# Cross-attention on one core: the attention product in seven block products, the softmax maximum as a bias

## The chip, the core and the metric

The kernel runs on one core of a Trainium2 chip. The metric is the device time of one execution in microseconds. Before the change the median of three runs is 286.38 us (286.36 to 286.68).

The engines are named as the profile names them: PE (TensorE, matmuls; PEld its weight loads), DVE (VectorE), ACT (ScalarE), POOL (GpSimd), SP (SyncE, which issues the DMAs). Each engine works through its own instructions in the order of the program and waits where an operand isn't ready.

## The reference

Everything is in fp32. There are 16 batches of 256 queries (width 256) and 77 keys (width 192), 8 heads of width 256. The output has the shape of x.

```python
Q = (img_embed @ Wq).reshape(B, -1, H, D).transpose(0, 2, 1, 3)
K = (sent_embed @ Wk).reshape(B, -1, H, D).transpose(0, 2, 1, 3)
V = (sent_embed @ Wv).reshape(B, -1, H, D).transpose(0, 2, 1, 3)
score = jnp.einsum('bhqd,bhkd->bhqk', Q, K) / math.sqrt(D)
score = jnp.where(mask, score, -jnp.inf)
attn = jax.nn.softmax(score, axis=-1)
ctx = jnp.einsum('bhqk,bhkd->bqhd', attn, V).reshape(B, -1, H * D)
out = ctx @ Wo + img_embed
mu = jnp.mean(out, axis=-1, keepdims=True)
var = jnp.var(out, axis=-1, keepdims=True)
return (out - mu) * jax.lax.rsqrt(var + EPS) * gamma + beta
```

## The kernel before

The weights are multiplied with each other first. Per head, g = Wk Wq^T (tiles gA and gB, the key width 192 split into 128 and 64 rows) and u = Wv Wo (uA and uB). With the keys' inputs c, a = g c gives the scores as x a, and vw = c u gives the output as a sum over heads of p vw. So the attention product of one batch is a matrix p of 256 queries by 8 x 77 keys times a matrix of 8 x 77 rows by 256 columns. Of each head 64 keys go into four blocks of 128 rows (two heads' halves to a block; the array runs in column strips of 32), and the 13 last keys of all heads go into a fifth block, vr.

After a preparation of some 57 us a loop runs over b from -1 to 15, one step for each batch, as a pipeline by hand: in step b the two query tiles (of 128 queries) of batch b + 1 are "new", those of batch b are "now", those of batch b - 1 are "old". Each engine's order is the program's:

- `scores(t)` (L297), PE: x times a for a new tile, 32 groups of four matmuls of 154 columns over two tiles (two records each, as fp32 goes through in two passes).
- `finish(t)` (L374, L376, L379), DVE: adds the product in PSUM to x and takes mean and variance. `spread` (L387), ACT: the root. `invert` (L394), DVE: its reciprocal.
- `shift(t)` (L311, L318, L319): DVE adds the mask's bias to the scores and takes the maximum `top`; POOL subtracts the maximum.
- `exponential(t)` (L326), ACT: one activation for a tile of 8 x 77. Root and exponential need different tables, so each step has two table loads on ACT.
- `prepare_vw(b + 1)` (L225, L236) and, in the steps up to b = 10, `prepare_a` for a part of the next group of four batches (L184, L198), PE; their copies from PSUM to SBUF are ACT's (L752, L754).
- `weigh(t)` (L332, L334, L340): DVE sums the exponentials and inverts the sum, POOL multiplies.
- `normalise(t)` (L416, L419), DVE; from the twelfth step on partly ACT and POOL instead (L412 to L414). Then SP sends the result (L427).
- `transpose_x` (L160), DVE, in two steps of each group of four; `turn_last` (L287), DVE, in the first half of the loop.
- `attend(t)` (L362), PE: the product for a "now" tile, five blocks by four strips of 256 columns. `turn(t)` (L350), DVE, transposes p of the new tiles for the next step's product.

All PSUM tiles share eight banks; a matmul into a bank waits until its last reader is done.

Of the kernel before, what the change touches and what calls it, by code (L numbers as in the profile page):

```python
# [8 lines left out]
F32 = mybir.dt.float32  # L9
# [6 lines left out]
P = 128  # L16
H = 8
D = 256
EPS = 1e-05
GB = 4  # L20
KM = 64
MASKED = 3.0e38

# [19 lines left out]
def kernel(  # L45
# [51 lines left out]

    gB = const.tile([P, NF, DI], F32, tag="gB", name="gB")

    uA = const.tile([P, 2, DI // BK, NF, BK], F32, tag="uA", name="uA")  # L100
    uB = const.tile([P, 2, DI // BK, NF, BK], F32, tag="uB", name="uB")

    cA = const.tile([P, B, S2], F32, tag="cA", name="cA")
    cB = const.tile([P, B, S2], F32, tag="cB", name="cB")
# [110 lines left out]

    def prepare_vw(b):

        vw_of[b] = vwp.tile([P, 2, 2, DI], F32, tag="vw", name=f"vw_{b}", bufs=3)
        pv = []

        def part_A():
            for k in range(2):
                pv.append(ps_mm.tile([P, 2 * DI], F32, tag="mm", name=f"pv_{b}_{k}"))
                for i in range(NM):
                    nc.tensor.matmul(  # L225
                        pv[k][i * BK : (i + 1) * BK],
                        cA[:, b, k * BK : (k + 1) * BK],
                        uA[:, :, :, i],
                        start=True,
                        stop=False,  # L230
                    )

        def part_B():
            for i in range(NM):
                for k in range(2):
                    nc.tensor.matmul(  # L236
                        pv[k][i * BK : (i + 1) * BK],
                        cB[half(k), b, k * BK : (k + 1) * BK],
                        uB[half(k), :, :, i],
                        start=False,  # L240
                        stop=True,
                    )

        def copies():
            return [
                (vw_of[b][:, :, k, :], pv[k].rearrange("p (e d) -> p e d", e=2)) for k in range(2)
            ]

        return part_A, part_B, copies

    def prepare_last():


        pr = [ps_mm.tile([P, 2, B, KR], F32, tag="mm", name=f"pr_{n}") for n in range(DI // BK)]

        def part_A(e):
            for n, o in enumerate(pr):
                nc.tensor.matmul(  # L258
                    o[:, e].rearrange("p b k -> p (b k)"),
                    flat(uA[:, e, n]),  # L260
                    flat(cRA),
                    start=(e == 0),
                    stop=(e == 1),
                )

        def part_B(e):
            for n, o in enumerate(pr):
                nc.tensor.matmul(  # L268
                    o[:, e].rearrange("p b k -> p (b k)"),
                    flat(uB[half(n % 2), e, n]),  # L270
                    flat(cRB[half(n % 2)]),
                    start=(e == 1),
                    stop=(e == 0),
                )

        part_A(0)
        part_B(0)
        part_B(1)
        part_A(1)
        for n, o in enumerate(pr):  # L280
            to = vr[:, :, n * BK : n * BK + 2 * KR]
            evacuate(to.rearrange("p b (e k) -> p e b k", e=2), o)
# [22 lines left out]

    def shift(t):

        b, ps = t // QT, ps_of.pop(t)
        s = sp.tile([P, H, S2], F32, tag="s", name=f"s_{t}")
        for a in range(2):  # L310
            nc.vector.tensor_tensor(  # L311
                s[:, a * H // 2 : (a + 1) * H // 2],
                ps[a][:, : H // 2 * S2].rearrange("p (h k) -> p h k", k=S2),
                bias[:, b, :].unsqueeze(1).to_broadcast([P, H // 2, S2]),
                ALU.add,
            )
        top = st.tile([P, H], F32, tag="top", name=f"top_{t}")
        nc.vector.tensor_reduce(top, s, AX.X, ALU.max)  # L318
        nc.gpsimd.tensor_tensor(  # L319
            s, s, top.unsqueeze(2).to_broadcast([P, H, S2]), ALU.subtract  # L320
        )
        s_of[t] = s

    def exponential(t):
        e = sp.tile([P, H, S2], F32, tag="e", name=f"e_{t}")
        nc.scalar.activation(e, s_of.pop(t), AF.Exp)  # L326
        e_of[t] = e

    def weigh(t):
# [27 lines left out]
    def attend(t):  # L357
        b, pT = t // QT, pT_of.pop(t)
        po = ps_mm.tile([P, DI], F32, tag="mm", name=f"po_{t}")
        for n in range(NF + 1):  # L360
            for i in range(NM):
                nc.tensor.matmul(  # L362
                    po[i * BK : (i + 1) * BK],
                    pT[:, n, i],
                    vw_of[b][:, n // 2, n % 2, :] if n < NF else vr[:, b, :],
                    start=(n == 0),
                    stop=(n == NF),
                )
        po_of[t] = po

    def finish(t):
        g, j = t // GT, t % GT
        y = xg_of[g][:, j, :]
        nc.vector.tensor_tensor(y, po_of.pop(t), y, ALU.add)  # L374
        bn = st.tile([P, 6], F32, tag="bn", name=f"bn_{t}")
        nc.vector.bn_stats(bn, y)  # L376
        if j == 0:
            mv_of[g] = st.tile([P, GT, 2], F32, tag="mv", name=f"mv_{g}", bufs=2)
        nc.vector.bn_aggr(mv_of[g][:, j, :], bn)  # L379
# [54 lines left out]
    with tc.tile_pool(name="wonce", bufs=1) as wp:  # L434
# [247 lines left out]
        for j in range(NF // 2):  # L682
            pu = two_banks("pu", j)
            for a in range(2 * j, 2 * j + 2):
                of_pair(pu, a, wv_part, wo_part)
            for e in range(2):
                evacuate(
                    uA[:, e, :, 2 * j : 2 * j + 2].rearrange("p n a c -> p a n c"),
                    pu[e].rearrange("p a (n c) -> p a n c", c=BK),
                )  # L690
        for j in range(NF // 2):
            for e, pw in enumerate(
                rest_of_pairs(j, (2 * j, 2 * j + 1), wv_part, wo_part, "pw")
            ):
                for i, engine in enumerate((nc.scalar.copy, nc.vector.tensor_copy)):
                    a = 2 * j + i
                    here, there = uB[half(i), e, :, a], uB[half(1 - i), e, :, a]
                    engine(here, pw[half(i)].rearrange("p (n c) -> p n c", c=BK))
                    nc.gpsimd.tensor_copy(there, here)
        nan = wp.tile([P, B, 1], F32, tag="nan", name="nan")  # L700
        nc.vector.tensor_reduce(nan[:, :, 0], bias, AX.X, ALU.max)
        nc.gpsimd.tensor_tensor(nan, nan, nan, ALU.mult)
# [16 lines left out]
    for b in range(-1, B):  # L719
        old = range(max(b - 1, 0) * QT, b * QT)  # L720
        now = range(max(b, 0) * QT, (b + 1) * QT)
        new = range((b + 1) * QT, min(b + 2, B) * QT)
        for t in new:
            scores(t)
        if old and new:
            for t in old:
                finish(t)
            spread(old[0], old[-1] + 1)
        for t in new:
            shift(t)  # L730
        for n in range(0, 2) if b < 0 else range(b + 2, min(b + 3, B // 2)):
            turn_last(n)
        if old and new:
            invert(old[0], old[-1] + 1, aside=b >= B - GB - 1)
        g, n = (b + 1) // GB + 1, (b + 1) % GB
        work = []
        if b + 1 < B:
            work.append(prepare_vw(b + 1))
        if g < NG:
            work.append(prepare_a(g, (n,)))  # L740
            if n == 0:
                load_xT(g)
                load_x(g)
        for part_A, _, _ in work:
            part_A()
        for _, part_B, _ in work:
            part_B()
        copies = [copy for _, _, of_part in work for copy in of_part()]
        for i, t in enumerate(new):
            exponential(t)  # L750
            for dst, src in copies[i : i + 1]:
                nc.scalar.copy(dst, src)  # L752
        for dst, src in copies[len(new) :]:
            nc.scalar.copy(dst, src)  # L754
        for i, t in enumerate(new):
            weigh(t)
            if old and b < B - 2 and (i or b < B - GB - 1):
                normalise(old[i])
        if g < NG and n >= NF - 2:
            for j in range((n - NF + 2) * GT // 2, (n - NF + 3) * GT // 2, 2):  # L760
                transpose_x(g, j)
        for t in now:
            attend(t)
        for t in new:
            turn(t)
        if B - GB - 1 <= b < B - 2:
            normalise(old[0], aside=True)
        if b == B - 2:
            for i in range(QT):
                normalise(old[i], aside=True)  # L770
                finish(now[i])
            spread(now[0], now[-1] + 1)
# [43 lines left out]
```

## Time and profile before

| | |
|---|---|
| median of 3 runs | 286.38 us |
| the profiled execution | 285.98 us |
| its span, first to last instruction | 284.2 us |
| granted PE clock | 0.996 |
| first scores of the loop, on PE | 57.30 us |
| step b = 1 begins on PE | 82.10 us |
| step b = 11 begins on PE | 226.97 us |
| scores of the last batch end on PE | 265.28 us |
| a step of b = 1 to 10, PE | 14.49 us |
| a step of b = 11 to 13, PE | 11.38 us |

The span is divided by the chain of work into a preparation (to 57.3 us), seventeen steps and a tail of some 16 us after 268.1, in which the last tiles go through exponential, product and normalisation one after the other.

A row of the groups of instructions reads: line, engine, operation, output <- inputs, shapes, count, then busy time, the mean of one in ns, and the idle time before them with what ended it. A row of the stretches reads: stretch, length, and then busy time and count for PE, PEld, DVE, ACT and POOL.

### The profile page before, as it was taken

The page shows a single profiled execution, that of the slowest core. Times are in us where ns is not written, and L with a number is a line of the kernel's source. Part 1 is how long each engine was busy: PE and PEld are TensorE (multiplying, and loading weights), DVE is VectorE, ACT ScalarE, POOL GpSimd, SP SyncE. Part 2 cuts the span into 40 slices and gives each one's busy share as a digit, 9 for nine tenths or more (in the row PEclk, how much of TensorE's full clock was granted, in tenths as well). Part 3 has the DMA queues.
Part 4 walks back from the last instruction along what each step waited for, and adds up shares of the span by engine and source line. Part 5 has one row for each costly group of instructions (what it writes and reads, how often), then busy time and mean ns, then how long its engine had stood idle before and what let it go on. Part 6 is the DMA issues. An engine that isn't in the chain of part 4 may idle for free.

```text
span 284.2 us, 11523 instructions
## 1 busy us (share of the span) xinstructions
PE 274.4 (97%) x5221; PEld 180.2 (63%) x5221; DVE 215.3 (76%) x421; ACT 115.2 (41%) x199; POOL 119.1 (42%) x150
## 2 busy tenths in 40 slices
PE   8999999999999999999999999999999999999990
PEld 7746599976474747575656565666656567476550
DVE  0245953775777989988888888897978898898883
ACT  3303222214362444453535353535353534725541
POOL 1000069524515252525252434352533437748574
PEclk9999999999999999999999999999999999999998
DMA  6997999960000105920101039301010101010112
GB/s 211 229 224 174 325 213 225 155 142 2 2 6 2 40 2 102 189 86 5 39 2 40 2 81 193 105 2 39 3 39 5 40 3 39 2 42 3 39 40 74
DMA packets 35634, 22.51 MB, mean 79 GB/s; under 512 B 17712, under 2 KB 34048, under 8 KB 35584
## 3 DMA queue, kind: packets, MB, share of 16 engines
q1 hardware_dynamic: 35584, 21.77, 34.8%
q8 instruction: 41, 0.67, 1.0%
q14 instruction: 9, 0.07, 0.1%
HBM read 17.57 MB, written 4.19 MB: 77 GB/s over the span
## 4 chain that ended last, share of the span: by engine, by line
PE 93%; DVE 2%; POOL 1%; ACT 1%; issue 1%; POOLq 0%
PE ps L297 24%; PE po L362 22%; PE pa L184 12%; PE pv L225 10%; PE pa L198 6%; PE pv L236 6%; PE pu L568 3%; PE pr L258 2%; PE pg L611 1%; PE idle L493 1%; PE pw L582 1%; PE pgb L568 1%; PE pr L268 1%; PE pc L545 1%; PE phb L582 1%; PE ph L625 1%
## 5 line engine op out<-in xcount | busy, mean ns | idle before, releaser
L319 POOL TENSOR_TENSOR s<-s,top 128x616 f32<-128x616 f32 x32 | 38.9, 1216 | 90.5 <-DVE top L318 86.0
L297 PE MATMUL ps<-a,xT 128*32 128x154 f32 x2048 | 70.0, 294 | 0.0
L297 PEld LDWEIGHTS ps<-a,xT 128*32 128x32 f32 x2048 | 66.4, 110 | 3.5 <-issue 0.7
L340 POOL TENSOR_TENSOR p<-e,rden 128x512 f32<-128x512 f32 x64 | 50.1, 802 | 31.8 <-ACT a L754 27.0
L362 PE MATMUL po<-vw,pT 128*32 128x256 f32 x1024 | 61.5, 380 | 0.0
L362 PEld LDWEIGHTS po<-vw,pT 128*32 128x32 f32 x1024 | 31.8, 110 | 28.2 <-issue 5.5
L332 DVE TENSOR_REDUCE den<-e 128x8 f32<-128x616 f32 x32 | 25.3, 790 | 23.6 <-ACT e L326 23.6
L184 PE MATMUL pa<-cA,gA 128*32 128x308 f32 x512 | 35.8, 423 | 0.4 <-ACT cA L136 0.4
L326 ACT ACTIVATE e<-s 128x616 f32<-128x616 f32 x32 | 23.0, 719 | 28.7 <-POOL s L319 28.7
L752 ACT COPY vw<-pv 128x512 f32<-128x512 f32 x32 | 18.6, 581 | 36.1 <-PE pv L236 36.1
L311 DVE TENSOR_TENSOR s<-ps,bias 128x308 f32<-128x308 f32 x64 | 27.8, 465 | 4.1 <-PE ps L297 4.1
L225 PE MATMUL pv<-uA,cA 128*32 128x512 f32 x256 | 30.4, 592 | 0.0
L184 PEld LDWEIGHTS pa<-cA,gA 128*32 128x32 f32 x512 | 16.4, 110 | 21.1 <-issue 6.1
L419 DVE SCALAR_TENSOR_TENSOR xg<-xg,rstd,bet 128x256 f32<-128x256 f32 x25 | 27.9, 1117 | 0.9
L387 ACT ACTIVATE std<-mv,eps 128x2 f32<-128x2 f32 (+1 forms) x17 | 5.0, 296 | 55.1 <-DVE mv L379 54.3
L350 DVE STREAM_TRANSPOSE pT<-p 128x640 f32<-128x640 f32 x32 | 25.0, 811 | 2.5 <-POOL p L340 2.5
L318 DVE TENSOR_REDUCE top<-s 128x8 f32<-128x616 f32 x32 | 25.5, 796 | 1.1
L362 PE MATMUL po<-vr,pT 128*32 128x256 f32 x256 | 19.7, 379 | 0.0
L198 PE MATMUL pa<-cB,gB 64*32 64x308 f32 x512 | 19.5, 420 | 0.0
L387 ACT ACT_TABLE_LOAD x15 | 19.2, 1283 | 0.3
L326 ACT ACT_TABLE_LOAD x14 | 18.0, 1283 | 0.3
L236 PE MATMUL pv<-uB,cB 64*32 64x512 f32 x256 | 17.4, 601 | 0.0
(86 smaller groups left out, 272.2 us busy)
## 6 DMA issues: line engine op xcount, KB each, us to landing
xT<-in_x_dram SPq DMA_DIRECT2D x16, 256.0 KB, 7.4
xg<-in_x_dram SPq DMA_DIRECT2D x4, 1024.0 KB, 9.0
out_dram<-xg SPq DMA_DIRECT2D x15, 256.0 KB, 2.2
wo<-in_L_xattn_Wo_dram SPq DMA_DIRECT2D x4, 512.0 KB, 5.4
wvT<-in_L_xattn_Wv_dram SPq DMA_DIRECT2D x16, 96.0 KB, 3.9
wq_nat<-in_L_xattn_Wq_dram SPq DMA_DIRECT2D x2, 512.0 KB, 6.1
wq_blk<-in_L_xattn_Wq_dram SPq DMA_DIRECT2D x8, 128.0 KB, 4.4
wk_blk<-in_L_xattn_Wk_dram SPq DMA_DIRECT2D x8, 96.0 KB, 5.8
```

The lines of the kernel that those rows point to most:

```text
L184: nc.tensor.matmul(flat(o[i * BK : (i + 1) * BK]), gA[:, h, cols(dc, i)], flat(cA[:, batches, :]), start=not B_first, stop=B_first,)
L198: nc.tensor.matmul(flat(banks[j + k][i * BK : (i + 1) * BK]), gB[half(k), h % NF, cols(dc, i)], flat(cB[half(k), batches, :]), start=B_fir ...
L225: nc.tensor.matmul(pv[k][i * BK : (i + 1) * BK], cA[:, b, k * BK : (k + 1) * BK], uA[:, :, :, i], start=True, stop=False,)
L236: nc.tensor.matmul(pv[k][i * BK : (i + 1) * BK], cB[half(k), b, k * BK : (k + 1) * BK], uB[half(k), :, :, i], start=False, stop=True,)
L297: nc.tensor.matmul(ps[m // 2][i * BK : (i + 1) * BK, m % 2 * 2 * S2 : (m % 2 + 1) * 2 * S2], xT_of[g][:, j * NM + m, dc], flat(a_of[g][:, ...
L311: nc.vector.tensor_tensor(s[:, a * H // 2 : (a + 1) * H // 2], ps[a][:, : H // 2 * S2].rearrange("p (h k) -> p h k", k=S2), bias[:, b, :]. ...
L318: nc.vector.tensor_reduce(top, s, AX.X, ALU.max)
L319: nc.gpsimd.tensor_tensor(s, s, top.unsqueeze(2).to_broadcast([P, H, S2]), ALU.subtract)
L326: nc.scalar.activation(e, s_of.pop(t), AF.Exp)
L340: nc.gpsimd.tensor_tensor(part, e_mh[:, :, :, keys], rden_mh.unsqueeze(3).to_broadcast(list(part.shape)), ALU.mult,)
L362: nc.tensor.matmul(po[i * BK : (i + 1) * BK], pT[:, n, i], vw_of[b][:, n // 2, n % 2, :] if n < NF else vr[:, b, :], start=(n == 0), stop= ...
L419: nc.vector.scalar_tensor_tensor(y, y, rstd, bet, ALU.mult, ALU.add)
```

## The change

For the batches 0 to 10 (b < NS, NS = 11) the product of p and vw is done in the form of Strassen (Winograd's variant). p of a batch is seen as two query tiles by two halves of the blocks, vw as two halves of the blocks by two halves of the 256 columns. In place of eight block products of 128 columns there are seven, plus products with the fifth block vr, which are added to four of them in PSUM. The sums that the form needs are made so: the one for the right-hand side, `t2`, comes out of the projection, since uA and uB get a fifth slice with the sum of slices (four additions on POOL in the preparation); the differences `ts` and `vd` of vw and vr (`differences`) and the four sums of p (`sums`) are POOL's in each step; the products land in two PSUM tiles, pm and po, and `add_seven` has ACT copy pm to SBUF and POOL add it to x in five additions. The second query tile's `finish` then reads only 128 columns from PSUM.

For the tiles of batches 0 to 11 the maximum is taken with its sign turned and goes in as the bias of the exponential, which so becomes eight activations of 77 columns, one for each head; POOL's subtraction is left out there.

The steps b < 11 have an order of their own: each old tile's `finish` stands ahead of a new tile's `shift`, the root comes after both exponentials, the copies after the root, the transpositions of x between the two `weigh`, and DVE normalises the first old tile before `turn` and the second after it. The later steps are as before. No DMA is added or taken away.

```diff
-    uA = const.tile([P, 2, DI // BK, NF, BK], F32, tag="uA", name="uA")
-    uB = const.tile([P, 2, DI // BK, NF, BK], F32, tag="uB", name="uB")
+    NH = DI // 2 // BK
+    uA = const.tile([P, 5, NH, NF, BK], F32, tag="uA", name="uA")
+    uB = const.tile([P, 5, NH, NF, BK], F32, tag="uB", name="uB")
+    NS = B - GB - 1
...
     def prepare_vw(b):
-        vw_of[b] = vwp.tile([P, 2, 2, DI], F32, tag="vw", name=f"vw_{b}", bufs=3)
+        vw_of[b] = vwp.tile([P, 4, 2, P], F32, tag="vw", name=f"vw_{b}", bufs=3)
+        parts = slice(0, 4) if b < NS else slice(1, 5)
...
-                        uA[:, :, :, i],
+                        uA[:, parts, :, i],
...
     def shift(t):
...
-        nc.vector.tensor_reduce(top, s, AX.X, ALU.max)
-        nc.gpsimd.tensor_tensor(
-            s, s, top.unsqueeze(2).to_broadcast([P, H, S2]), ALU.subtract
-        )
-        s_of[t] = s
+        nc.vector.tensor_reduce(top, s, AX.X, ALU.max, negate=t // QT <= NS)
+        if t // QT > NS:
+            nc.gpsimd.tensor_tensor(
+                s, s, top.unsqueeze(2).to_broadcast([P, H, S2]), ALU.subtract
+            )
+        s_of[t] = s, top
 
     def exponential(t):
         e = sp.tile([P, H, S2], F32, tag="e", name=f"e_{t}")
-        nc.scalar.activation(e, s_of.pop(t), AF.Exp)
+        s, top = s_of.pop(t)
+        if t // QT > NS:
+            nc.scalar.activation(e, s, AF.Exp)
+        else:
+            for h in range(H):
+                nc.scalar.activation(e[:, h], s[:, h], AF.Exp, bias=top[:, h : h + 1])
         e_of[t] = e
...
+    def differences(b):
+        vw = vw_of[b].rearrange("p q k d -> p q (k d)")
+        ts = vwp.tile([P, 3, 2, P], F32, tag="ts", name=f"ts_{b}", bufs=2)
+        nc.gpsimd.tensor_tensor(
+            ts.rearrange("p q k d -> p q (k d)"),
+            vw[:, 1:4],
+            vw[:, 0:1].to_broadcast([P, 3, 2 * P]),
+            ALU.subtract,
+        )
+        vd = vwp.tile([P, P], F32, tag="vd", name=f"vd_{b}", bufs=2)
+        nc.gpsimd.tensor_tensor(vd, vr[:, b, :P], vr[:, b, P:], ALU.subtract)
+        ts_of[b] = ts, vd
+
+    def sums(b):
...
+        ss = vwp.tile([P, 4, 2, NM, BK], F32, tag="ss", name=f"ss_{b}", bufs=2)
+        s1, s3, s2, s4 = (ss[:, i].rearrange("p k m q -> p (k m q)") for i in range(4))
+        nc.gpsimd.tensor_tensor(s1, a2[0], a2[1], ALU.add)
+        nc.gpsimd.tensor_tensor(s3, a2[0], a1[0], ALU.subtract)
+        nc.gpsimd.tensor_tensor(s2, a2[1], s3, ALU.add)
+        nc.gpsimd.tensor_tensor(s4, a1[1], s2, ALU.subtract)
+        ss_of[b] = ss
+
+    def seven(b):
...
+        contract(pm[:, 0], pT[0][:, 0:2], b11)
+        contract(pm[:, 1], s2, t2)
+        contract(pm[:, 2], s3, t3, (pT[1][:, NF], ends[1]))
+        contract(pm[:, 3], s1, t1)
+        contract(po[:, 0], pT[0][:, 2:4], b21, (pT[0][:, NF], ends[0]))
+        contract(po[:, 1], s4, b22, (pT[0][:, NF], ends[1]))
+        contract(po[:, 2], pT[1][:, 2:4], t4, (pT[1][:, NF], vd))
+        po_of[QT * b] = flat(po[:, 0:2]), slice(None)
+        po_of[QT * b + 1] = po[:, 2], slice(P)
+        pm_of[b] = pm
+
+    def add_seven(b):
+        m = vwp.tile([P, 4, P], F32, tag="m", name=f"m_{b}", bufs=1)
+        nc.scalar.copy(m, pm_of.pop(b))
+        j = QT * b % GT
+        y = xg_of[QT * b // GT][:, j : j + QT].rearrange("p t (c d) -> p t c d", c=2)
+
+        def add(to, what):
+            nc.gpsimd.tensor_tensor(to, to, what, ALU.add)
+
+        add(m[:, 1], m[:, 0])
+        add(y[:, 0], m[:, 0:2])
+        add(y[:, :, 1], m[:, 3:4].to_broadcast([P, QT, P]))
+        add(m[:, 2], m[:, 1])
+        add(y[:, 1], m[:, 2:3].to_broadcast([P, 2, P]))
...
+        for u in (uA, uB):
+            t2, _, b22, b11, b12 = (u[:, q].rearrange("p n i c -> p (n i c)") for q in range(5))
+            nc.gpsimd.tensor_tensor(t2, b22, b12, ALU.subtract)
+            nc.gpsimd.tensor_tensor(t2, t2, b11, ALU.add)
...
+        if b < NS:
+            for i, t in enumerate(new):
+                if old:
+                    finish(old[i])
+                shift(t)
...
+        if b < NS:
+            for i, t in enumerate(new):
+                exponential(t)
+                if i and old:
+                    spread(old[0], old[-1] + 1)
+                weigh(t)
+                if i == 0 and n >= NF - 2:
+                    for j in range((n - NF + 2) * GT // 2, (n - NF + 3) * GT // 2, 2):
+                        transpose_x(g, j)
+            for dst, src in copies:
+                nc.scalar.copy(dst, src)
+            if b + 1 < NS:
+                differences(b + 1)
+            if now:
+                seven(b)
+                add_seven(b)
+            if old:
+                invert(old[0], old[-1] + 1)
+                normalise(old[0])
+            for t in new:
+                turn(t)
+            if b + 1 < NS:
+                sums(b + 1)
+            if old:
+                normalise(old[1])
+            continue
```

`contract(out, weights, moving, ...)` issues, for each block of 128 rows, four matmuls of 128 columns, one for each strip of 32 columns of the array.

More of the change, by code (lines that the diff above doesn't have):

```diff
@@ L98, with of_e @@
     gB = const.tile([P, NF, DI], F32, tag="gB", name="gB")
-    uA = const.tile([P, 2, DI // BK, NF, BK], F32, tag="uA", name="uA")
-    uB = const.tile([P, 2, DI // BK, NF, BK], F32, tag="uB", name="uB")
+    NH = DI // 2 // BK
+    uA = const.tile([P, 5, NH, NF, BK], F32, tag="uA", name="uA")
+    uB = const.tile([P, 5, NH, NF, BK], F32, tag="uB", name="uB")
+    NS = B - GB - 1
+    def of_e(u, e):
+        return u[:, 3 - 2 * e : 5 - 2 * e].rearrange("p q n i c -> p (q n) i c")
     cA = const.tile([P, B, S2], F32, tag="cA", name="cA")
@@ L238, in part_B @@
                         cB[half(k), b, k * BK : (k + 1) * BK],
-                        uB[half(k), :, :, i],
+                        uB[half(k), parts, :, i],
                         start=False,
@@ L245, in copies @@
             return [
-                (vw_of[b][:, :, k, :], pv[k].rearrange("p (e d) -> p e d", e=2)) for k in range(2)
+                (vw_of[b][:, :, k, :], pv[k].rearrange("p (q d) -> p q d", q=4)) for k in range(2)
             ]
@@ L259, in part_A @@
                     o[:, e].rearrange("p b k -> p (b k)"),
-                    flat(uA[:, e, n]),
+                    flat(of_e(uA, e)[:, n]),
                     flat(cRA),
@@ L269, in part_B @@
                     o[:, e].rearrange("p b k -> p (b k)"),
-                    flat(uB[half(n % 2), e, n]),
+                    flat(of_e(uB, e)[half(n % 2), n]),
                     flat(cRB[half(n % 2)]),
@@ L364, in attend @@
                     pT[:, n, i],
-                    vw_of[b][:, n // 2, n % 2, :] if n < NF else vr[:, b, :],
+                    vw_of[b][:, 2 - n // 2 * 2 : 4 - n // 2 * 2, n % 2, :] if n < NF else vr[:, b, :],
                     start=(n == 0),
@@ L368, in attend @@
                 )
-        po_of[t] = po
+        po_of[t] = po, slice(None)
+    def differences(b):
[10 more added lines that the diff above has]
+        ts_of[b] = ts, vd
@@ new lines, in sums @@
+    def sums(b):
+        a1, a2 = (
+            [flat(pT_of[QT * b + i][:, 2 * e : 2 * e + 2].rearrange("p n m q -> p n (m q)"))
+             for e in range(2)]
+            for i in range(QT)
+        )
+        ss = vwp.tile([P, 4, 2, NM, BK], F32, tag="ss", name=f"ss_{b}", bufs=2)
[5 more added lines that the diff above has]
+        ss_of[b] = ss
@@ new lines, in seven, with contract @@
+    def seven(b):
+        pT = [pT_of.pop(QT * b + i) for i in range(QT)]
+        vw, ss = vw_of[b], ss_of.pop(b)
+        ts, vd = ts_of.pop(b)
+        pm = ps_mm.tile([P, 4, P], F32, tag="mm", name=f"pm_{b}")
+        po = ps_mm.tile([P, 3, P], F32, tag="mm", name=f"po_{b}")
+        t2, b21, b22, b11 = (vw[:, q] for q in range(4))
+        t4, t1, t3 = (ts[:, q] for q in range(3))
+        s1, s3, s2, s4 = (ss[:, i] for i in range(4))
+        ends = vr[:, b, :P], vr[:, b, P:]
+        def contract(out, weights, moving, *last):
+            terms = [(weights[:, k], moving[:, k]) for k in range(2)] + list(last)
+            for n, (weight, moving) in enumerate(terms):
+                for i in range(NM):
+                    nc.tensor.matmul(
+                        out[i * BK : (i + 1) * BK],
+                        weight[:, i],
+                        moving,
+                        start=(n == 0),
+                        stop=(n == len(terms) - 1),
+                    )
+        contract(pm[:, 0], pT[0][:, 0:2], b11)
[8 more added lines that the diff above has]
+        pm_of[b] = pm
@@ L371, in finish @@
+    ts_of, ss_of, pm_of = {}, {}, {}
     def finish(t):
@@ L373, in finish @@
         y = xg_of[g][:, j, :]
-        nc.vector.tensor_tensor(y, po_of.pop(t), y, ALU.add)
+        po, cols = po_of.pop(t)
+        nc.vector.tensor_tensor(y[:, cols], po, y[:, cols], ALU.add)
         bn = st.tile([P, 6], F32, tag="bn", name=f"bn_{t}")
@@ L687 @@
                 evacuate(
-                    uA[:, e, :, 2 * j : 2 * j + 2].rearrange("p n a c -> p a n c"),
+                    of_e(uA, e)[:, :, 2 * j : 2 * j + 2].rearrange("p n a c -> p a n c"),
                     pu[e].rearrange("p a (n c) -> p a n c", c=BK),
@@ L696 @@
                     a = 2 * j + i
-                    here, there = uB[half(i), e, :, a], uB[half(1 - i), e, :, a]
+                    here, there = (of_e(uB, e)[half(k), :, a] for k in (i, 1 - i))
                     engine(here, pw[half(i)].rearrange("p (n c) -> p n c", c=BK))
                     nc.gpsimd.tensor_copy(there, here)
+        for u in (uA, uB):
+            t2, _, b22, b11, b12 = (u[:, q].rearrange("p n i c -> p (n i c)") for q in range(5))
+            nc.gpsimd.tensor_tensor(t2, b22, b12, ALU.subtract)
+            nc.gpsimd.tensor_tensor(t2, t2, b11, ALU.add)
         nan = wp.tile([P, B, 1], F32, tag="nan", name="nan")
@@ L724 @@
             scores(t)
-        if old and new:
+        if b < NS:
[3 more added lines that the diff above has]
+                shift(t)
+        elif new:
             for t in old:
@@ L728 @@
             spread(old[0], old[-1] + 1)
-        for t in new:
-            shift(t)
+            for t in new:
+                shift(t)
         for n in range(0, 2) if b < 0 else range(b + 2, min(b + 3, B // 2)):
             turn_last(n)
-        if old and new:
-            invert(old[0], old[-1] + 1, aside=b >= B - GB - 1)
+        if b >= NS and new:
+            invert(old[0], old[-1] + 1, aside=True)
         g, n = (b + 1) // GB + 1, (b + 1) % GB
@@ L748 @@
         copies = [copy for _, _, of_part in work for copy in of_part()]
+        if b < NS:
[17 more added lines that the diff above has]
+                normalise(old[0])
+            for t in new:
+                turn(t)
[4 more added lines that the diff above has]
+            continue
         for i, t in enumerate(new):
@@ L756 @@
             weigh(t)
-            if old and b < B - 2 and (i or b < B - GB - 1):
+            if old and b < B - 2 and i:
                 normalise(old[i])
-        if g < NG and n >= NF - 2:
-            for j in range((n - NF + 2) * GT // 2, (n - NF + 3) * GT // 2, 2):
-                transpose_x(g, j)
         for t in now:
@@ L765 @@
             turn(t)
-        if B - GB - 1 <= b < B - 2:
+        if b < B - 2:
             normalise(old[0], aside=True)
```

## The prediction

> **What bounds the kernel now.** I read the page's busy shares first, then the chain of waits in order of time, then the busy times by stage, then the timelines of VectorE, ScalarE and GpSimd over one batch.
>
> ```profile
> PE 274.4 (97%) x5221; PEld 180.2 (63%) x5221; DVE 215.3 (76%) x421; ACT 115.2 (41%) x199; POOL 119.1 (42%) x150
> ...
> 140.04 4.19 PE ps L297 x128
> 144.23 1.72 PE pv L225 x16
> 145.95 2.07 PE pa L184 x32
> 148.02 1.02 PE pv L236 x16
> 149.04 1.04 PE pa L198 x32
> 150.08 4.45 PE po L362 x80
> 154.53 4.19 PE ps L297 x128
> ...
> 140.04:154.53 14.49, 14.49 (x313) 9.02 (x308) 12.12 (x25) 6.53 (x11) 5.68 (x6) 1.00 0.07 22
> ```
>
> In the chain (second part: start, length, link) one step of the batch loop is PE alone, 4.19 + 1.72 + 2.07 + 1.02 + 1.04 + 4.45 = 14.49 us, with no gap, and the next step repeats it. The last line (stretch, length, busy PE, PEld, DVE, ACT, POOL) shows DVE at 12.12 of 14.49 in this step (13.19 in the fullest), ACT at 6.53, POOL at 5.68. So PE sets the pace, DVE comes next, ACT and POOL have more than half free.
>
> After the eleventh step PE has no more of "pa" to do and a step takes 11.38 us. There DVE is no follower with room to spare:
>
> ```profile
> 239.37 0.38 DVE L374 TENSOR_TENSOR xg<-po,xg 128x256 f32<-128x256 f32 x1
> ...
> 245.07 0.80 DVE L332 TENSOR_REDUCE den<-e 128x8 f32<-128x616 f32 x1 [0.41 <-ACT e L326]
> ...
> 250.65 0.38 DVE L374 TENSOR_TENSOR xg<-po,xg 128x256 f32<-128x256 f32 x1
> ```
>
> In DVE's timeline its first addition of a step (L374) comes every 11.28 us, and what it idles in between (0.41 and 0.57) is waiting for exponentials of its own scores. It wins back 0.1 us a step on PE; so a delay of DVE at step 11 arrives at the end nearly whole. In the trace of before that first addition of step 11 starts at 227.97.
>
> **What the skill says.** TensorE: Matmul & The Clock Gate, section LDWEIGHTS: a weight load costs its columns over 1.2 GHz, 27 ns for 32 columns. Here a load lasts 110 ns whatever moves behind it, four of them side by side, which agrees with 4 x 27. ScalarE: Activation LUTs, section What ACT_TABLE_LOAD costs: 1283 ns for a load (the trace has 1283), and 280 + 0.833 N ns for an ACTIVATE with a pointer bias, of which about 93 overlap with the next; the trace has 296 for N = 2 (L387), which agrees. SBUF — State Buffer, section Who interferes with whom: a DVE instruction with two SBUF inputs and a GpSimd one that reads SBUF exclude each other for the whole instruction. The timelines of the tail agree:
>
> ```profile
> 278.36 0.72 POOL L414 TENSOR_TENSOR xg<-xg,bet 128x256 f32<-128x256 f32 x1
> 278.40 0.96 DVE L416 SCALAR_TENSOR_TENSOR xg<-xg,mv,gam 128x256 f32<-128x256 f32 x1
> 279.04 0.90 POOL L413 TENSOR_TENSOR xg<-xg,gam 128x256 f32<-128x256 f32 x1
> 279.39 0.83 DVE L419 SCALAR_TENSOR_TENSOR xg<-xg,rstd,bet 128x256 f32<-128x256 f32 x1
> ```
>
> DVE's 0.43 us operation ends 0.28 us after the POOL operation it met; POOL's next one loses 0.17, the one after 0.05. In the loop the same L419 takes 1156 ns for the same reason.
>
> **PE, part by part.** Removed per batch: 20 passes of four matmuls of 256 columns (each fp32 matmul shows as two), 4.45 us. Added: 18 products of 128 columns in two passes, 36 passes. A pass takes 131 ns for 154 columns (4.19/32) and 430 for 512 (1.72/4): 0.835 ns a column and 2 over, so 109 ns for 128. The weight load (110) is then as long as the stream. Bounds: 109 (3.92 us) to 131, the shortest pass that the trace shows with such loads (4.72). I take 110: 3.96 us, 0.49 less per batch, eleven times 5.4 us. The PE step becomes 14.0. This is all the change can win; the exponent's bias and the sums are there to pay for it.
>
> **The other engines.** Removed: the subtraction on POOL (L319, 1.22 us, 24 times), and its hand-over between the maximum and the exponential. Added on ACT: 8 exponentials of 77 columns for one of 616 (0.72). One is 280 + 64 = 344 ns, then one every 0.251 by the skill; copies here overlap by 0.13, which would give 0.21. I take 0.24: sixteen take 3.96 us (3.5 to 4.1). Also the copy of pm, 0.58. Added on POOL per batch, from these rows:
>
> ```profile
> L319 POOL TENSOR_TENSOR s<-s,top 128x616 f32<-128x616 f32 x32 | 38.9, 1216 | 90.5 <-DVE top L318 86.0
> L340 POOL TENSOR_TENSOR p<-e,rden 128x512 f32<-128x512 f32 x32 | 35.4, 1107 | 31.8 <-ACT a L754 27.0 <-DVE rden L334 4.7
> ...
> L413 POOL TENSOR_TENSOR xg<-xg,gam 128x256 f32<-128x256 f32 x7 | 5.3, 756 | 0.3 <-ACT xg L412 0.3
> ```
>
> Undisturbed, L413 takes 0.73 for 256 columns and L319 1.22 for 616: some 0.19 plus 2.1 ns a column for two full inputs, 1.67 where one is repeated. The difference of 768 columns: 1.47 to 1.85, taken 1.7; vd 0.47; the five additions 0.47, 0.73, 0.73, 0.47, 0.73 and 0.08 for each wait on the one before; the four sums 3.2. POOL's work goes from 5.7 to about 11 us of 14: it fits, so capacity is not the point. Latency is, because every engine works in order.
>
> **The loop.** Count from S, where DVE starts the first addition of a step (finish of the old tile 0).
> - DVE: finish 0.97 (pitch in the trace), two additions and the maximum 1.69: top ready at 2.66.
> - ACT: before, the table load ran ahead while the exponential waited for POOL (at 142.26, exponential at 144.91). In the changed program the wait for top stands in front of the load, since the exponential now waits for three semaphores and only the last stays with it. Load 2.70 to 3.98, sixteen exponentials to 7.96 (the second tile's top, about 5.1, is in time). Then load and root to 9.55, two copies of vw to 10.6, four of a to 11.9, pm to 12.4. PE has pm ready by then.
> - DVE: den and reciprocal of tile 1 from 8.0 to 9.0 (0.3 later in the six steps with two transposes of x between the two dens).
> - POOL: p of tile 1 from 9.15, 1.38 undisturbed, so 10.55; difference and vd to 12.7; three additions with their waits (0.47 + 0.81 + 0.81) to 14.8. Behind DVE's four normalising instructions, which now fall into this stretch, POOL loses 0.05 to 0.2 each, with the restarts 0.6 in all (0 to 1.5): 15.4.
> - DVE: the next step's finish needs the third addition. So S returns after 15.4 us, against 14.0 for PE and 14.49 before.
>
> The PE stalls where pa and pm ask for PSUM banks that DVE frees late. Start: step 0 has neither root nor table load; PE ends its product at 81.6, the copy at 80.2 meets a POOL busy with the difference until 80.4, three additions: S for step 1 is 82.6. Then step 1 without a table load in front (14.1), eight of 15.4 (123.2), step 10 without difference (15.0), transposes 6 x 0.3 = 1.8: step 11's finish starts at 82.6 + 14.1 + 123.2 + 15.0 + 1.8 = 236.7, against 227.97: 8.7 us later, carried to the end as shown above. The four preparatory additions (5.2 us on POOL, idle from 54.3 to 61.0) only move the first shift by about 1 us, long before the first product at 77.6; price nothing, or 1 us without that cover. The DMAs are the same in number and size. The order of normalisation is changed within DVE; its output DMA leaves SP some microseconds later; behind it on SP stand only the loads of the next group's x, which is turned two steps later.
>
> The profiled execution took 285.98 us (span 284.2), the median 286.38. 286.4 + 8.7 gives 295.
>
> **Rivals.**
> 1. PE's saving shows: the loop stays within PE's 14.0, so the end moves by 5 us: 281.3. For it: POOL and ACT are half idle, and PE owns the chain. Against it: the sum above would have to be 1.4 too long; short exponentials (-0.45), no exclusion (-0.6) and a fast difference (-0.2) give 14.15. A smaller gain comes below 14.5. Chance 0.12 for both.
> 2. The exclusion costs whole instructions: each of DVE's four normalising instructions makes POOL wait its full 0.43, and the exponentials take 0.25 each: loop 16.5, 11 us more than forecast, 306. For it: L419's 1156; against: POOL lost only 0.05 to 0.17 in the tail. Chance 0.13.
> 3. Nothing comes of it: weight loads eat PE's gain (131 a pass, +0.27 a batch) and the loop stays at 14.5, or both about cancel: 286.4. Chance 0.04.
>
> **How the numbers follow.** The forecast has 0.71. The loop's bounds without rivals, 14.7 to 15.9, give 288 to 300. The range, 286 to 303, takes in rival 3 and part of 2; below it is rival 1. A measurement of this kernel can tell about 0.2% from no change. Faster 0.12, within 0.2% 0.04, slower 0.84.
>
> **What would show it.** PE gaps of about 1.4 us in steps 2 to 10, at pa or pm, released by DVE; a step of 15.4; ACT's load for the exponential starting only after top; 16 exponentials in about 4 us; POOL busy without a gap from p of tile 1 to the sums; L374 released by POOL. The product at 3.96 us a batch. The forecast is wrong if steps 2 to 10 take 14.0, if the load runs ahead of top, or if the product takes over 4.5 us and PE stays without gaps.

## The result, and the profile after

The changed kernel takes 298.74 us (median, 298.34 to 299.43), the kernel before 286.53 us beside it: a ratio of 1.0425, 95% interval 1.0397 to 1.0452. It is 12.2 us slower. The profiled execution took 298.41 us, its span is 296.6 us (284.2 before).

First the page of the changed kernel: busy shares, then the shares of the chain of waits by engine, then two groups of instructions.

```profile
PE 276.6 (93%) x5925; PEld 196.9 (66%) x5925; DVE 208.7 (70%) x421; ACT 150.4 (51%) x376; POOL 186.2 (63%) x251
...
DVE 27%; PE 26%; POOL 22%; ACT 18%; issue 4%; DMA 2%; POOLq 0%; SPq 0%; ACTq 0%; DVEq 0%
...
L349 ACT ACT_TABLE_LOAD x9 | 11.5, 1283 | 55.3 <-DVE top L335 55.3
...
L480 DVE TENSOR_TENSOR xg<-po,xg 128x256 f32<-128x256 f32 (+1 forms) x32 | 11.7, 364 | 22.2 <-POOL xg L466 22.1
```

PE fell from 97% to 93%, POOL went from 42% to 63%, ACT from 41% to 51%, and DVE even fell from 76% to 70%. So none has become the engine that is always busy. But the chain, 93% PE before, is now shared by four engines. The two groups name two of its links: before nine table loads ACT idled 55.3 us in all until the maximum was there, and before its first additions (L480) DVE idled 22.1 us for POOL.

The chain of waits in order of time (start, length, link), over one step of the changed kernel:

```profile
145.19 0.74 POOL xg L466
147.06 0.76 DVE s L328 x2
147.84 0.81 DVE top L335
148.73 1.28 ACT L349
150.03 1.13 ACT e L349 x5
151.29 0.85 ACT e L349 x3
152.16 0.81 DVE den L355
153.17 1.30 DVE xT L175 x2
154.48 0.69 DVE den L355
155.54 1.56 POOL p L363 x2
157.10 1.99 POOL ts L399
159.09 0.60 POOL vd L406
159.69 0.61 POOL m L466
160.37 0.74 POOL xg L466
161.18 0.74 POOL xg L466
```

This is the loop of the prediction, link for link: POOL's third addition ends, DVE's first addition of the next step starts at 145.95, maximum, table load, exponentials, sum, p, difference, vd, three additions, and DVE starts the next step at 161.95, 16.0 us later. In the step shown the transposition of x lies between the two sums, as was said for six steps. Over the eight steps from 98.48 to 225.40 the mean is 15.87 us; PE needs 14.1 and needed 14.49 before. (PE's steps 1 and 2 still take 14.1 us: PE is ahead of DVE at first, and its first gap in the loop stands at 123.27, at the end of step 3.) PE's timeline in the step shown tells who holds it up:

```profile
147.47 1.25 PE L199 MATMUL pa<-cA,gA 128*32 128x308 f32 x16 [0.37 <-DVE s L328]
148.88 0.72 PE L199 MATMUL pa<-cA,gA 128*32 128x308 f32 x8 [0.17 <-DVE xg L480]
...
156.26 4.00 PE L313 MATMUL ps<-a,xT 128*32 128x154 f32 x116 [0.53 <-ACT vw L874]
```

In brackets stands the idle time before a group and who ended it. PE waits for PSUM banks that DVE (shift, finish) and ACT (copy of vw) free late. Its gaps at those places are 1.07 us in this step, and 1.3 us in the next.

Step 11's first addition starts at 240.22 in the changed kernel and at 227.97 in the one before: 12.25 us later, and the span is 12.4 us longer. What was lost up to there arrived at the end whole.

### The profile page after: what moved, and what is told of

Its sections match the earlier page's. It is cut to its first block, busy times and chain, and to the rows that moved or that the text cites. A ratio compares the mean times of both kernels' runs of the same rounds, so it can differ in the third digit from the quotient of the medians.

```text
span 296.6 us, 13213 instructions
## 1 busy us (share of the span) xinstructions
PE 276.6 (93%) x5925; PEld 196.9 (66%) x5925; DVE 208.7 (70%) x421; ACT 150.4 (51%) x376; POOL 186.2 (63%) x251
## 4 chain that ended last, share of the span: by engine, by line
DVE 27%; PE 26%; POOL 22%; ACT 18%; issue 4%; DMA 2%; POOLq 0%; SPq 0%; ACTq 0%; DVEq 0%
ACT e L349 10%; POOL xg L466 5%; POOL ts L399 5%; DVE top L335 5%; DVE s L328 5%; POOL p L363 5%; PE ps L313 5%; PE pa L199 4%; DVE den L355 4%; ACT L349 3%; DVE bn L482 3%; PE pu L674 3%; DVE xg L480 2%; PE pa L213 2%; POOL m L466 2%
## 5 line engine op out<-in xcount | busy, mean ns | idle before, releaser
L313 PE MATMUL ps<-a,xT 128*32 128x154 f32 x2048 | 72.8, 295 | 5.0 <-ACT vw L874 2.7
L363 POOL TENSOR_TENSOR p<-e,rden 128x512 f32<-128x512 f32 x64 | 46.7, 751 | 46.6 <-DVE rden L357 45.3
L349 ACT ACTIVATE e<-s,top 128x77 f32<-128x77 f32 x192 | 49.5, 346 | 11.5 <-DVE top L335 11.4
L199 PE MATMUL pa<-cA,gA 128*32 128x308 f32 x512 | 38.3, 425 | 3.2 <-DVE s L328 2.0
L349 ACT ACT_TABLE_LOAD x9 | 11.5, 1283 | 55.3 <-DVE top L335 55.3
L480 DVE TENSOR_TENSOR xg<-po,xg 128x256 f32<-128x256 f32 (+1 forms) x32 | 11.7, 364 | 22.2 <-POOL xg L466 22.1
L466 POOL TENSOR_TENSOR xg<-xg,m 128x256 f32<-128x256 f32 x33 | 24.3, 736 | 2.6
L399 POOL TENSOR_TENSOR ts<-vw 128x768 f32<-128x768 f32 x11 | 21.9, 1994 | 0.0
L385 PE MATMUL po<-vw,pT 128*32 128x256 f32 x320 | 19.2, 380 | 0.7 <-DVE pT L373 0.7
L337 POOL TENSOR_TENSOR s<-s,top 128x616 f32<-128x616 f32 x8 | 9.7, 1218 | 14.3 <-DVE top L335 12.8
L522 DVE SCALAR_TENSOR_TENSOR xg<-xg,mv,gam 128x256 f32<-128x256 f32 x25 | 17.3, 690 | 0.0
```

The costliest lines, as they stand in the source:

```text
L199: nc.tensor.matmul(flat(o[i * BK : (i + 1) * BK]), gA[:, h, cols(dc, i)], flat(cA[:, batches, :]), start=not B_first, stop=B_first,)
L313: nc.tensor.matmul(ps[m // 2][i * BK : (i + 1) * BK, m % 2 * 2 * S2 : (m % 2 + 1) * 2 * S2], xT_of[g][:, j * NM + m, dc], flat(a_of[g][:, ...
L349: nc.scalar.activation(e[:, h], s[:, h], AF.Exp, bias=top[:, h : h + 1])
L363: nc.gpsimd.tensor_tensor(part, e_mh[:, :, :, keys], rden_mh.unsqueeze(3).to_broadcast(list(part.shape)), ALU.mult,)
L399: nc.gpsimd.tensor_tensor(ts.rearrange("p q k d -> p q (k d)"), vw[:, 1:4], vw[:, 0:1].to_broadcast([P, 3, 2 * P]), ALU.subtract,)
L466: nc.gpsimd.tensor_tensor(to, to, what, ALU.add)
```

## The experiments

The theory is the loop of waits. Its rivals are that POOL lacks time as a whole, that the short activations alone cost the time, and that DVE's exclusion of POOL costs whole instructions. Each ratio is to the kernel before, run beside that kernel: 286.53 us beside the changed one, about 287.5 beside the first four experiments, 287.1 beside the last two. So a difference of two rows in us can be off by 1 us, and the ratios are the better comparison. The step is the mean distance of DVE's first additions over the same eight steps of the profiled execution. What the new order of the steps costs by itself, with the eight products, was not run.

| kernel | us | ratio to before, interval | step |
|---|---|---|---|
| changed | 298.74 | 1.0425, 1.0397 to 1.0452 | 15.87 |
| additions first | 290.55 | 1.0116, 1.0071 to 1.0161 | 14.98 |
| table load ahead | 291.97 | 1.0164, 1.0142 to 1.0186 | 15.07 |
| both | 284.41 | 0.9893, 0.9870 to 0.9917 | 14.26 |
| no bias | 296.09 | 1.0308, 1.0287 to 1.0328 | 15.43 |
| bias alone, on before | 289.09 | 1.0066, 1.0041 to 1.0090 | 14.49 |
| no normalising | 292.32 | 1.0179, 1.0119 to 1.0238 | 15.17 |

### Additions before differences

```diff
-            if b + 1 < NS:
-                differences(b + 1)
             if now:
                 seven(b)
                 add_seven(b)
+            if b + 1 < NS:
+                differences(b + 1)
```

> Edit: POOL does the five additions of add_seven before the differences of the next batch; the work is the same. Theory (a loop of waits through DVE, ACT, POOL sets the step): the additions no longer stand behind ts (1.99 us) and vd (0.60), only behind the copy of m, which ends 12.5 us after the step's first L480; three additions and their waits are 2.1 us, so a step is 14.7 us for 15.9, and ten steps give about 12 us back: 286 to 288. Rival (POOL is short of time as a whole, through its own work and DVE's exclusion): the order moves nothing, 297 to 300.

290.55 us, 8.2 less than the changed kernel, with the same work for every engine. So time on POOL as a whole isn't what lacks: the first rival falls. POOL's timeline of this kernel:

```profile
155.46 0.46 POOL L466 TENSOR_TENSOR m<-m 128x128 f32<-128x128 f32 x1 [1.43 <-ACT m L461]
155.99 1.67 POOL L466 TENSOR_TENSOR xg<-xg,m 128x256 f32<-128x256 f32 x2
```

POOL now idles 1.43 us until ACT has copied pm: the link before the additions is ACT, not ts and vd. Seven of the eight steps are 14.8 us, near the 14.7 expected; the eighth is 16.1, for a gap of PE told of at the end. The expectation counted ten such steps, but step 10 has no differences to put behind the additions: it takes 14.82 us in both kernels. (So the changed kernel has itself a step without differences ahead of the additions, and it is as short as those of this run.) These two steps, and a start 1.0 us later than in the changed kernel (PE's first scores come as much later, before anything that was edited), are most of what lacks of the 12 us.

### The table load ahead of the wait

```diff
                 seven(b)
                 add_seven(b)
+            if old and b + 1 < NS:
+                ahead = st.tile([P, GT], F32, tag="std", name=f"ahead_{b}")
+                nc.scalar.activation(ahead[:, :1], eps, AF.Exp)
```

> Edit: after the copy of pm, ACT does an exponential of one column that nobody reads, so the table load stands ahead of the wait for the maximum. Theory (loop of waits): the 1.28 us of the load leave the loop in nine steps, a step is 14.6 us, nine times 1.28 is 11.5: 287. Rival (POOL is short of time): 298, unchanged. Rival (what costs is the eight-fold activation itself, 4.1 us of ACT for 1.4): ACT gets one instruction more, unchanged or 0.2 us a step slower.

291.97 us, 6.8 less, with one instruction more: the load was in the loop, and the rival that blames the activations themselves would have given nothing. But the gain is little more than half of the 11.5 expected. ACT's timeline says where the rest stayed:

```profile
147.40 2.11 ACT L349 ACTIVATE e<-s,top 128x77 f32<-128x77 f32 x8 [4.57 <-DVE top L335]
149.85 2.11 ACT L349 ACTIVATE e<-s,top 128x77 f32<-128x77 f32 x8 [0.35 <-DVE top L335]
```

Counted from the step's first addition, the first tile's exponentials start 1.28 us sooner (2.80 for 4.08), and the second tile's then wait 0.35 us for their own maximum. A step without transpositions fell from 15.79 to 14.96 us. With the transpositions of x it depends on the step. In two of the four, where `turn_last` (L303) stands ahead of them too, they end 0.5 to 0.6 us after the last exponential (0.2 to 0.35 in the changed kernel) and the step is 15.29 and 15.41 us; in the other two they end no later than the exponentials, and the step is 14.95 and 14.96. A new wait took the place of part of the old one.

### Both

> Edit: the two edits (additions before differences, table load ahead) together. Theory: the loop of waits falls to 13.4 us, below PE's 14.1 (10.04 and the product's 4.06), so PE sets the step again and the saving of the product shows: ten steps of 14.1 to 14.4 for 14.49 before, 282 to 285. Rivals: as in the single edits, 296 to 300.

284.41 us: 1.1% faster than the kernel before and 14.3 us faster than the changed one. The chain in order of time, of this kernel:

```profile
96.99 4.19 PE ps L313 x128
101.18 1.72 PE pv L241 x16
102.89 2.07 PE pa L199 x32
104.97 1.02 PE pv L252 x16
105.98 1.04 PE pa L213 x32
107.02 2.10 PE pm L439 x72
109.12 1.97 PE po L439 x72
111.09 4.19 PE ps L313 x128
```

PE sets the step again, 14.10 us here, and the product costs 4.07 where it cost 4.45. This is what the seven products can win here, and it shows only when the loop beside PE is shorter than PE's step. POOL's busy share of such a step, by stage (stretch, length, PE, PEld, DVE, ACT, POOL, then granted clock, DMA share and GB/s):

```profile
98.07:112.17 14.10, 14.10 (x376) 10.37 (x372) 12.88 (x27) 10.09 (x27) 11.20 (x16) 1.00 0.07 22
```

POOL does its 11.2 us in this step of 14.1 without holding up PE.

### The bias undone, and the bias alone

Undone in the changed kernel:

```diff
-            for h in range(H):
-                nc.scalar.activation(e[:, h], s[:, h], AF.Exp, bias=top[:, h : h + 1])
+            nc.scalar.activation(e, s, AF.Exp)
```

and POOL's subtraction is back in `shift`.

> Edit: the bias of the exponential is undone (POOL subtracts the maximum again, one exponential per tile), the seven products stay. Theory: in the loop the table load and sixteen exponentials (1.28 + 4.11 us after the maximum) give way to POOL's sums, which it must end first, two subtractions of 1.22 and two exponentials of 0.72: the second exponential is ready about 7.5 us after the first L480 for 8.2, in the six steps with transposes less is won; 292 to 297. Rival (the bias with its short activations is what costs): 286 to 289. Rival (POOL is short of time): 2.44 us more a batch on POOL, so over 305.

296.09 us: 2.7 less than the changed kernel (by the ratios 1.2% of the time before, some 3.4 us), within what was expected. Steps with transpositions stay at 15.7 to 15.9, the others fall to 15.0 to 15.1. POOL does 2.4 us more a batch and the kernel is faster; the bias by itself is the smaller part of the loss.

The same bias, for the batches 0 to 11, in the kernel before:

> Edit: the kernel before with nothing but the bias: for batches 0 to 11 the maximum goes in as the bias of eight exponentials and POOL's subtraction is left out; order and product are those of before. Theory (a part costs what it adds to a loop of waits, and nothing while that loop is shorter than PE's 14.49): DVE's loop with the table load and the longer exponentials in it is 13.9 us in steps without transposes of x and 15.2 with them; the six long steps lose at most 0.7 each and DVE's spare time of the others takes back some of it: 286 to 291. Rival (the bias with its short activations is what costs the 12 us): over 294.

289.09 us, 0.7% slower than before. ACT's timeline:

```profile
145.60 1.28 ACT L332 ACT_TABLE_LOAD   x1 [1.34 <-DVE top L318]
146.90 2.11 ACT L332 ACTIVATE e<-s,top 128x77 f32<-128x77 f32 x8
```

The load waits for the maximum here too. But the loop does not set the step. PE's scores follow each other by 14.49 us as before, with no gap:

```profile
169.65 4.19 PE ps L297 x128
...
184.14 4.19 PE ps L297 x128
```

DVE's first additions are 13.6, 13.9, 15.7 and 14.8 us apart in each group of four steps, and 13.3, 14.5, 15.7 and 14.5 in the kernel before; the mean is PE's 14.49 in both. So no step lost the up to 0.7 us of the expectation: its range was met for another reason. What is lost is a lag, paid once. The first addition of step 1, before and with the bias:

```profile
81.29 0.39 DVE L374 TENSOR_TENSOR xg<-po,xg 128x256 f32<-128x256 f32 x1
```

```profile
83.34 0.38 DVE L380 TENSOR_TENSOR xg<-po,xg 128x256 f32<-128x256 f32 x1
```

It is 2.05 us later, of which 0.64 lies ahead of the loop (PE's first scores start at 57.94 for 57.30); at step 11 it is 2.35 us later (230.32 for 227.97), and the span is 2.3 us longer. While PE sets the step, the longer way through DVE and ACT moves DVE behind PE once here, and doesn't add up from step to step.

### DVE's normalisation left out

In the tiles of batches 0 to 10 the four instructions of a step at L522 and L525, DVE's normalisation, are left out.

> Edit: the changed kernel without DVE's four normalising instructions in the tiles of batches 0 to 10 (these rows go out unnormalised). Theory (DVE's two-input instructions lengthen the POOL operations that they meet, inside the loop): p of the second tile falls from 1.56 to 1.38 us, ts from 1.99 to 1.83, vd and the first addition from 0.61 to 0.46 each, a step from 15.9 to 15.2, the time by about 6 us to 292 to 294. Rival (POOL's lengths have another reason, such as the operands' layout): the four lengths stay and the time stays within 1 us of 298.7. Rival (exclusion takes whole instructions): a step below 14.5, under 287.

292.32 us, and a step of 15.17 for 15.87. The groups of POOL between 85 and 225 us, first of the changed kernel, then of this one (line, operation, shapes, count, busy us, mean ns):

```profile
L399 POOL TENSOR_TENSOR ts<-vw 128x768 f32<-128x768 f32 x9 | 18.2, 2028 | 0.0
...
L363 POOL TENSOR_TENSOR p<-e,rden 128x104 f32<-128x104 f32 x18 | 8.3, 459 | 0.0
...
L406 POOL TENSOR_TENSOR vd<-vr 128x128 f32<-128x128 f32 x9 | 5.8, 643 | 0.0
```

```profile
L399 POOL TENSOR_TENSOR ts<-vw 128x768 f32<-128x768 f32 x9 | 16.5, 1833 | 0.2
...
L363 POOL TENSOR_TENSOR p<-e,rden 128x104 f32<-128x104 f32 x18 | 6.6, 368 | 0.0
...
L406 POOL TENSOR_TENSOR vd<-vr 128x128 f32<-128x128 f32 x9 | 4.2, 461 | 0.0
```

A POOL operation that meets one of DVE's two-input instructions takes 0.18 to 0.20 us longer (the 104 columns come twice a step, undisturbed the first time, so their mean moves by half). The first of the additions, 0.64 us in the changed kernel, takes 0.46. The four together are the 0.7 us by which the step is shorter: that is what the exclusion costs the loop, not the 0.43 per instruction of rival 2.

## Why the prediction was right

The forecast was 295 in a range of 286 to 303; measured were 298.7. Its terms against the trace of the changed kernel:

| term of the sum | forecast | measured |
|---|---|---|
| first addition of step 1 | 82.6 | 83.07 |
| step 1 | 14.1 + 0.3 | 15.41 |
| eight steps with their transpositions | 123.2 + 1.2 | 126.92 |
| step 10 | 15.0 + 0.3 | 14.82 |
| first addition of step 11 | 236.7 | 240.22 |
| product on PE, per batch | 3.96 | 4.06 |

(The 1.8 us for six steps with transpositions lie here where they belong, 0.3 in step 1, 1.2 in the eight and 0.3 in step 10.) The measured time is 3.7 us above the forecast. The mechanism was right; what was off are sizes, and some of them hid others.

- That the loop through DVE, ACT and POOL would take the bound from PE was right, and both halves of it are shown: moving the additions or the load, with the work all but unchanged, shortens the step, and the two together give it back to PE.
- The table load behind the wait for the maximum was right (the load starts at 148.73, 0.09 us after the maximum's end at 148.64; all nine loads waited so); its price was shown by the run with the load ahead only in part, as the second maximum then comes late.
- The second tile's maximum was called "in time". In step 1, which has no load in front, it isn't: its exponentials start at 88.31, after an idle 0.34 us of ACT, since the maximum of the second tile ended at 88.20:

```profile
88.31 2.11 ACT L349 ACTIVATE e<-s,top 128x77 f32<-128x77 f32 x8 [0.34 <-DVE top L335]
```

This is 0.34 of the 1.0 us by which the sum was too short in step 1. The sizes of the next point are further parts of it; the remainder was not separated.
- Three sizes were too small in the eight regular steps, and one too large (2.5 us in all). Sixteen exponentials take 4.11 us, not 3.96: one every 0.251, so the price of the Trainium skill (ScalarE: Activation LUTs, What ACT_TABLE_LOAD costs) was the better one and the copies' overlap the wrong neighbour. And ts, 1.83 undisturbed, was taken at 1.7: with the prediction's fixed 0.19 that is 2.1 ns a column, so the repetition of a block of 256 columns costs as much as a full second input; only L319's repetition of one element is cheaper (1.67). With 0.6 for the exclusion, measured at 0.7, these are 0.15 + 0.13 + 0.1 = 0.38 us a step. The four steps without transpositions of x show it: 15.8 us for the 15.4 of the sum. The four with them take 15.87 to 16.0, so the transpositions cost 0.1 to 0.2 us, not 0.3, which takes back some 0.6 us over the eight. Step 10 was 0.5 us too long in the sum: without the differences it lasts the 14.8 us of the run with the additions first.
- The product on PE was nearly right: 4.06 us are 36 passes of 113 ns, for 110. Its bound from above (131) was far off. (A pass is one record in each of the four strips. The scores of a step are 64 matmuls of two records, so 32 passes; the list of the kernel before has them as 32 groups of matmuls.)
- PE's gaps were expected in steps 2 to 10. They come from the end of step 3 on, 1.1 to 1.3 us in the steps looked at for 1.4 forecast, because PE starts the loop ahead of DVE.
- The exclusion for the whole instruction, which the prediction cites and reads in the tail, does not show in full on POOL's side: POOL lost 0.05 to 0.17 us to DVE's 0.43 in the tail and 0.18 to 0.20 in the loop. The sum took the measured losses, not the rule, and so came close.
- The end: 12.25 us at step 11 became 12.4 us of span. That DVE wins back nothing in the last steps was right.

Rival 1 (PE's saving shows) did not hold for this change, but its mechanism was real: it is what the version with both edits does, from a loop below 14.1 us on. Rival 3 is out with the changed kernel's time. Of rival 2, the exclusion of whole instructions is out with the run without normalisation; its exponentials, one every 0.25 us, came true.

## What to carry to other kernels

When a change takes work from the bound engine and gives it to idle ones, add up latency, not busy time: follow one loop from an engine's first instruction of a step back to the same instruction of the next step, through every queue on the way, and compare the sum with the bound engine's step. In that loop, the order within each queue (what stands ahead of the result that is waited for) and the place of an unconditional instruction such as a table load (ahead of a wait or behind it) are worth as much as the durations. When one link is taken out, look at once for the wait that is next, here the second tile's maximum and the transpositions.

## What the runs showed of the hardware that was not expected

PE stops once for a time in the second half of the loop, in all six kernels with seven products and in neither of the two with eight. No semaphore in the profile releases it; the view calls it "issue". In the kernel with the additions first:

```profile
183.60 0.70 PE L313 MATMUL ps<-a,xT 128*32 128x154 f32 x15
186.78 5.66 PE L313 MATMUL ps<-a,xT 128*32 128x154 f32 x113 [2.48 <-issue]
```

The DMA records name a likely reason. One queue, q8, carries packets of 16 KB of the kind "instruction". There are 41 of them in the kernel before, where PE and PEld have about 10,450 records, and 46 in the changed one with 11,850: a packet for each 256 or so. In all six kernels PE goes on 1.3 to 1.4 us after such a packet has ended:

| kernel | PE stops | packet of q8 | PE goes on | gap |
|---|---|---|---|---|
| changed | 188.86 | 187.87 to 189.07 | 190.43 | 1.57 |
| additions first | 184.30 | 184.28 to 185.42 | 186.78 | 2.48 |
| table load ahead | 185.79 | 185.14 to 186.23 | 187.63 | 1.84 |
| both | 182.11 | 180.28 to 181.50 | 182.93 | 0.82 |
| no bias | 188.00 | 187.98 to 189.12 | 190.46 | 2.46 |
| no normalising | 175.36 | 173.86 to 174.97 | 176.30 | 0.94 |

In the first five the stop is before the same record of PE. In the sixth it is 256 matmuls and 256 weight loads earlier, which is just two packets. And in the microseconds before, the load of the next x keeps the DMA engines over 0.9 busy for 4 us or more; the packet comes when that ends. So PE seems to have run out of instructions, because their fetch came late behind the load of x. The step with seven products needs them faster: 748 records in 14.1 us, against 621 in 14.49 before. This is read from the traces alone. No run moved the load of x, and other packets come as late (8 us after the one before) without a stop.

After the two gaps of about 2.5 us the granted clock was 0.70 and 0.69 over the 5.5 us that follow; after the shorter ones it was 1.00. With the additions first the same 113 records so took 5.66 us for 3.98, and that is the step of 16.1.
